# Audio tower on one core: the last token tile's values by seven half-size products, and the token sums of the next group moved forward

## The chip, the core and the metric

The kernel runs on one core of a Trainium2 chip. A core has TensorE (PE, matrix products), VectorE (DVE), ScalarE (ACT), GpSimd (POOL) and SyncE (SP, which here only issues transfers). The engines run side by side, each in the order of its own instructions, and wait for one another through semaphores. The metric is the device time of one execution in microseconds (us).

## The reference, cut to what matters

64 clips of 80000 samples are cut into 157 frames of 512. A cosine transform makes `h` (64 x 157 x 512). Then come one attention layer and one layer of 16 experts, all in 32-bit floats:

```python
h = einsum('bfh,kh->bfk', frames, D)              # the tokenizer
x = layernorm(h)
key_phase = tanh(x @ Wk + bk) * pi                # query_phase alike
V = x @ Wv + bv
# phases and positions give causal weights over the tokens of one clip;
# V is summed with them, and gate = sigmoid(x @ Wg + bg) mixes the two sums
h = h + x + (total / norm) @ Wo + bo
y = layernorm(h)
# the mean of y over a clip's tokens chooses one of 16 experts for the clip
h = h + gate * (y @ We[idx] + be[idx])
```

The change concerns `V = x @ Wv + bv` alone, for some of the tokens.

## The kernel before, in words

**Groups and tiles.** The 64 clips go through in 16 groups (`g`) of four. A clip's 157 tokens are padded to 160, so a group has 640 token columns. They make five tiles: `n` = 0 to 3 with 128 columns each (32 tokens of each of the four clips), and a fifth, `TAIL`, which also has 128. The transposed input `xT` keeps them as two halves of 320 columns: half 0 holds tiles 0 and 1 and 64 columns of `TAIL`, half 1 the other 64 columns of `TAIL` and then tiles 2 and 3.

**Products.** A 512 x 512 weight on two halves of tokens is cut into two by two blocks, and the eight block products are replaced by seven (Strassen's scheme). `weight_sums` (L370) makes the sums of weight blocks once, `factors` (L384) names them 1 to 7. `token_sums` (L399) makes four sums of token blocks for each group, as a generator that stops after each sum: sum 0 (L411) and sum 2 (L414) on POOL or DVE, sums 1 and 3 (L99) always on DVE. `product` (L437) is one of the seven on 256 tokens, eight rows in the profile (line L445). `gather` (L455) puts it where it belongs. The gate uses all 320 columns of a half (`gate_product`, L648). The values use 256 of 320: `TAIL` doesn't take part in the seven, and is done by `value` (L486) with `by_tokens` (L247, matmuls L250): four matmuls with 512 columns. `keep_value` (L490) adds the bias `bv` on its way out (L100, DVE). Each row of a 32-bit matmul in the profile is one of two passes, so four matmuls are eight rows.

**Column tiles.** Where the stationary operand has 32 columns only, four matmuls stand side by side in the array, each on 32 of the 128 output partitions: the projection to phases (`project`, L594, matmuls L601), the scores (L689) and the experts (L953).

**Order.** It is written out by hand: each engine does its instructions in the order of the program. For each group from 1 on: `project_and_values` (L1098), `gate` (L1153), `experts_and_embedding` (L1171), `attention` (L1197). In the first, the projection is followed on PE by product 1, the tail values, and products 2, 6, 7, 5, 4, 3. Between them stand the steps that route the clips of the group before: `move_blocks` (L795) issues sixteen transfers, ten from SP and six from POOL, of the transposed tokens; `xsum`, `route`, `route_own`, `route_all`, `pick` make the choice on DVE; `fetch` (L893) issues four indirect loads of 1 MB from POOL. `fold_phases` (L611) and `phasors` (L615) turn the projected phases into sines on DVE and ACT. `add_bv` (L513) adds the bias to the values of tiles 0 to 3 on POOL.

**Where the token sums of the next group were made.** `attention(g)` ends with the output product, during which `scale_all` (L344) scales the next group's `xT`, with statistics (DVE, then POOL: L237 to L244), with the normalisation (`normal2`, ACT), then `value_sums(g + 1)` (L1190), which makes sums 0 and 2 on POOL, and `turn_blocks` (L787, DVE transposes) around two experts of the group before (`expert`, L973, with L964 on DVE). Sums 1 and 3 follow in the next `project_and_values`, behind `value`.

**Accumulators.** The pool of PSUM tiles has four buffers of two banks, taken in turn. Products 2, 4 and 3 are accumulated onto the buffers of 1, 7 and 5 (`ONTO`).

Of the kernel before, what the change touches and what calls it, by code (L numbers as in the profile page):

```python
# [17 lines left out]
ALU = mybir.AluOpType  # L18
# [4 lines left out]
P = 128  # L23
# [30 lines left out]
def audio_tower(ctx: ExitStack, tc: tile.TileContext, a, out):  # L54
# [36 lines left out]
    def psum():  # L91

        return ps_mm.tile([P, 2, 512], F32, tag="mm", name="mm")
# [153 lines left out]
    def by_tokens(ps, x, n, w):  # L247

        for c in range(C):
            nc.tensor.matmul(ps, tile_of(x[:, c], n), w[:, c, :], start=(c == 0), stop=(c == C - 1))  # L250
        return ps
# [73 lines left out]
    def add_bo(g, n):  # L325
        r = S[g]["res"][n]
        nc.gpsimd.tensor_tensor(r, r, bo, ALU.add)  # L327
# [16 lines left out]
    def scale_all(g):  # L344

        s = S[g]
        if g == 0:
            scale = psum()
            lo = 0

            for n in (0, 1, TAIL, TAIL, 2, 3):
                rows = slice(0, P) if n != TAIL else slice(0, HT) if lo < HN - 1 else slice(HT, P)
                m, at = divmod(lo, HN)
                w = rows.stop - rows.start
                nc.tensor.transpose(
                    scale[:, m, at : at + w], s["rstd", n][rows].to_broadcast([w, P]), ident[rows, rows]
                )
                lo += w
        else:
            scale = s.pop("scale")  # L360
        for m in range(2):
            x = half(s["xT"], m)
            nc.vector.tensor_tensor(x, x, scale[:, m, :HN].unsqueeze(1).to_broadcast([P, C, HN]), ALU.mult)
# [112 lines left out]
    def value_buffer(g, n):  # L476

        s = S[g]
        if n == TAIL:
            s["v", n] = p1.tile([P, D], F32, tag="v_t", name="v_t")  # L480
        else:
            s["v2", n // 2] = v = p1.tile([P, 2, D], F32, tag="v", name="v", bufs=2)
            for b in range(2):
                s["v", n + b] = v[:, b, :]

    def value(g, n):  # L486
        s = S[g]
        s["vps", n] = by_tokens(psum()[:, 0, :], s["xT"], n, wv)

    def keep_value(g, n):  # L490
        s = S[g]
# [21 lines left out]
    def add_bv(g, m, of=slice(0, D)):  # L513
        v = S[g]["v2", m][:, :, of]
        by = bv[:, of].unsqueeze(1).to_broadcast([P, 2, of.stop - of.start])
        nc.gpsimd.tensor_tensor(v, v, by, ALU.add)  # L516
# [255 lines left out]
    def normal2(g, n):  # L772
        s = S[g]
        if n == TAIL:
            x = p1.tile([P, D], F32, tag="v_t", name="x2_t")
        else:
            if n % 2 == 0:
                s["x22"] = p1.tile([P, 2, D], F32, tag="v", name="x2", bufs=2)
            x = s["x22"][:, n % 2, :]
        rstd, shift = s.pop(("st2", n))  # L780
        if at_end(g, n):
            nc.vector.tensor_scalar(x, s["res"][n], shift, rstd, ALU.subtract, ALU.mult)
        else:
            nc.scalar.activation(x, s["res"][n], AF.Identity, bias=shift, scale=rstd)  # L784
        s["x2", n] = x

    def turn_blocks(g, n):  # L787

        s = S[g]
        if n == TAIL:  # L790
            s["blocks2"] = p1.tile([P, C * GB, LP], F32, tag="gT", name="turned2")
        to = s["blocks2"].rearrange("p (q c) t -> p c q t", c=C)[..., Q * n : Q * (n + 1)]
        nc.vector.transpose(to, s.pop(("x2", n)).rearrange("p (c q t) -> p c q t", c=C, q=GB))
# [179 lines left out]
    def expert(g, n, between=lambda c: None):  # L973
        ps = psum()
        for c in range(C):
            between(c)
            expert_chunk(g, n, c, ps[:, 0, :])
        between(C)
        expert_out(g, n, ps[:, 0, :])
# [118 lines left out]
    def project_and_values(g):  # L1098

        project(g)  # L1100
        made = S[g].pop("made")
        if g == 1:
            turn_blocks(0, TAIL)
            turn_blocks(0, 2)
        fold_phases(g)
        if g == 1:
            turn_blocks(0, 3)
        value_product(g, 1)
        keep_product(g)
        if g == 1:  # L1110
            normal2(0, 0)
            normal2(0, 1)
        value(g, TAIL)
        next(made)
        if g == 1:
            for n in (2, 3, TAIL):
                add_bo(g, n)
            turn_blocks(0, 0)
        else:
            next(made)  # L1120
        keep_value(g, TAIL)
        if g == 1:
            turn_blocks(0, 1)
        moves = move_blocks(g - 1)
        next(moves)
        S[g - 1]["late"] = xsum(g - 1, 2 * Q, L)
        value_product(g, 2)
        keep_product(g)
        add_bv(g, 0, slice(0, H))
        next(moves)  # L1130
        phasors(g)
        value_product(g, 6)
        keep_product(g)
        route(g - 1)
        value_product(g, 7)
        keep_product(g)
        route_own(g - 1)
        value_product(g, 5)
        keep_product(g)
        if g == 1:  # L1140
            next(made)
        fold_once(g + 1, 0)
        value_product(g, 4)
        keep_product(g)
        route_all(g - 1)
        pick(g - 1)
        fetch(g - 1)
        value_product(g, 3)
        keep_product(g)
        weigh()  # L1150
        fold_twice(g + 1, 0)

    def gate(g):  # L1153
        ahead = g + 1 < NG
        for i in (1, 6, 2, 7, 5, 4, 3):
            gate_product(g, i)
            if i == 1:
                pick_gate(g - 1)
                bias(g - 1)
                fold_once(g + 1, 1)  # L1160
                add_bv(g, 0, slice(H, D))
                add_bv(g, 1)
            if i == 5:
                if not ahead:
                    scores(g)
                fold_twice(g + 1, 1)
            for n in {6: (0,), 2: (1,), 3: (2, 3, TAIL)}.get(i, ()) if ahead else ():
                embed(g + 1, n)
                embed_statistics(g + 1, n)
# [20 lines left out]
    def value_sums(g):  # L1190

        S[g]["blocks"] = halves(S[g]["xT"])
        S[g]["made"] = made = token_sums(g, engine=nc.gpsimd)
        next(made)
        next(made)

    def attention(g):  # L1197
        ahead = g + 1 < NG
        if ahead and g > 0:
            for n in (0, 1, 2):  # L1200
                add_bo(g + 1, n)
        if g == 0:
            for _ in weight_sums(wg, t_g, nc.gpsimd):
                pass
        for c in range(C):
            read(g, c)
            if ahead and g > 0:
                for n in ((), (3, TAIL), (), ())[c]:
                    add_bo(g + 1, n)
        S[g]["blocks"] = halves(S[g]["gT"])  # L1210
        made = token_sums(g, tail=False)
        if g == 0:
            for n in (0, 1):
                add_bo(1, n)
        for i in (1, 2, 6, 7, 5, 4, 3):
            output_product(g, i)
            if i == 1:
                for _ in range(4 if g else 3):
                    next(made)
                if g == 0:  # L1220
                    scale_all(1)
                output_tail(g)
                statistics2(g, (TAIL,))
            elif i == 6:
                normal2(g, TAIL)
            elif i == 7 and g == 0:
                next(made)
            elif i == 5 and g == 0:
                value_sums(1)
            elif i == 5 and ahead:  # L1230
                scale_all(g + 1)
        for of in ((0, 1),) if ahead else ((0,), (1,)):
            statistics2(g, of)
        normal2(g, 2)
        normal2(g, 3)
        if not ahead:
            normal2(g, 0)
        elif g > 0:
            normal2(g, 0)
            normal2(g, 1)  # L1240
            value_sums(g + 1)
            for n in (TAIL, 2, 3):
                turn_blocks(g, n)
            expert(g - 1, 2)
            for n in (0, 1):
                turn_blocks(g, n)
            expert(g - 1, 3)

    for g in range(NG):
        if g == 0:  # L1250
            first_values()
            first_gate()
        else:
            project_and_values(g)
            gate(g)
            if g + 1 < NG:
                experts_and_embedding(g)
            else:
                S[g]["rwg"] = rwg = p2.tile([P, C, Q], F32, tag="sines", name="rwg")
                nc.sync.dma_start(out=rwg, in_=a["rwg"])  # L1260
        attention(g)
# [160 lines left out]
```

## Time and profile before

| | us |
|---|---|
| median of three runs | 1302.68 |
| the runs | 1301.87 to 1304.14 |
| the profiled execution | 1301.98 |
| its span, first to last instruction | 1300.0 |
| PE busy | 1293.2 (99%) |
| DVE busy | 1023.6 (79%) |
| POOL busy | 592.7 (46%) |
| ACT busy | 431.9 (33%) |

The busy time of an engine counts from the first to the last of the instructions that overlap, so it tells that PE always had something in flight, not that each was at its best rate. The chain of work that ended last runs over PE for 97% of the span. The page is followed by groups of instructions (by line, engine and shape), waits (who waited for whom) and a timeline in order of time.

### The profile page before, as it was taken

How to read it: one execution, taken by the hardware profiler on the slowest of the kernel's cores; microseconds unless marked ns; L12 is line 12 of the kernel's file. 1: busy time of each engine (PE TensorE's matmuls, PEld its weight loads, DVE VectorE, ACT ScalarE, POOL GpSimd, SP SyncE). 2: the span in 40 equal slices, each digit the busy share in tenths (PEclk: the TensorE clock that was granted, in tenths of full speed). 3: DMA queues.
4: the chain of work that ended last, by engine and by line, in shares of the span. 5: the costliest groups of instructions: out<-in, count | busy, mean ns of one | idle time of the engine just before them, and what ended most of it. 6: DMA issues, size and time to landing. Idle time of an engine off the chain costs nothing.

```text
span 1300.0 us, 26072 instructions
## 1 busy us (share of the span) xinstructions
PE 1293.2 (99%) x10152; PEld 864.7 (67%) x10152; DVE 1023.6 (79%) x2056; ACT 431.9 (33%) x768; POOL 592.7 (46%) x781
## 2 busy tenths in 40 slices
PE   9999999999999999999999999999999999999998
PEld 5677666676666767666676666766666676666762
DVE  6888787878877887788878878788778877888583
ACT  2525334142432324334242331424323243342410
POOL 2356445344553446435444453446434454354424
PEclk9999999999999999999999999999999999999999
DMA  7015224252442425323252342424323262241506
GB/s 242 1 52 178 76 61 173 61 171 75 114 147 54 152 75 177 93 57 146 80 183 76 77 174 49 166 75 131 128 64 145 75 193 77 58 154 36 181 9 210
DMA packets 60578, 144.46 MB, mean 111 GB/s; under 512 B 14136, under 2 KB 31432, under 8 KB 52520
## 3 DMA queue, kind: packets, MB, share of 16 engines
q1 hardware_dynamic: 45620, 62.68, 17.6%
q0 software_dynamic: 14336, 79.47, 17.2%
q8 instruction: 81, 1.33, 0.4%
q10 hardware_dynamic: 500, 0.64, 0.2%
q14 instruction: 41, 0.34, 0.1%
HBM read 102.47 MB, written 20.62 MB: 95 GB/s over the span
## 4 chain that ended last, share of the span: by engine, by line
PE 97%; DMA 1%; POOL 1%; issue 0%; SPq 0%; DVE 0%; POOLq 0%
PE mm L445 29%; PE mm L953 20%; PE mm L658 17%; PE mm L250 10%; PE mm L705 9%; PE mm L270 3%; PE mm L272 3%; PE mm L601 3%; PE mm L637 1%; PE mm L689 1%; DMA tables<-in_table_sums 1%; DMA t_v<-in_we,rows 1%; PE mm L201 0%; PE mm L219 0%; PE mm L684 0%
## 5 line engine op out<-in xcount | busy, mean ns | idle before, releaser
L953 PE MATMUL mm<-we,x2T 128*32 128x512 f32 x2400 | 263.8, 593 | 0.0
L953 PEld LDWEIGHTS mm<-we,x2T 128*32 128x32 f32 x2400 | 75.0, 110 | 165.6 <-issue 165.5
L237 POOL TENSOR_SCALAR rstd<-mv 128x2 f32<-128x2 f32 (+1 forms) x50 | 11.7, 235 | 241.0 <-DVE mv L233 240.9
L516 POOL TENSOR_TENSOR v<-v,bv 128x512 f32<-128x512 f32 (+1 forms) x45 | 72.7, 1632 | 101.2 <-ACT v L465 101.2
L705 PE MATMUL mm<-att,v 32*128 32x320 f32 (+3 forms) x2048 | 113.2, 357 | 0.0
L705 PEld LDWEIGHTS mm<-att,v 32*128 32x128 f32 x2048 | 94.6, 185 | 22.0 <-issue 12.6
L784 ACT ACTIVATE x<-res,shift,rstd 128x512 f32<-128x512 f32 x61 | 46.4, 807 | 172.7 <-POOL shift L244 171.9
L327 POOL TENSOR_TENSOR res<-res,bo 128x512 f32<-128x512 f32 x64 | 95.7, 1514 | 13.1 <-ACT res L323 13.0
L100 DVE TENSOR_TENSOR gT<-mm,gT 128x320 f32<-128x320 f32 (+3 forms) x128 | 71.2, 566 | 31.7 <-PE mm L658 28.7
L712 DVE TENSOR_TENSOR gT<-mm,gT 128x320 f32<-128x320 f32 x128 | 59.5, 485 | 42.4 <-PE mm L705 42.3
L237 POOL TENSOR_SCALAR dev<-mv 128x5 f32<-128x5 f32 (+1 forms) x20 | 4.9, 244 | 188.7 <-DVE mv L233 188.1
L232 DVE BATCH_NORM_STATS2 st<-res 128x6 f32<-128x512 f32 x128 | 87.9, 686 | 3.3
L445 PE MATMUL mm<-t_o,sum 128*128 128x256 f32 x384 | 85.5, 379 | 0.0
L445 PE MATMUL mm<-t_v,sum 128*128 128x256 f32 x360 | 80.1, 379 | 0.0
L445 PEld LDWEIGHTS mm<-t_o,sum 128*128 128x128 f32 x384 | 73.0, 190 | 9.9
L676 ACT ACTIVATE gT<-gT,hbg 128x320 f32<-128x320 f32 (+1 forms) x90 | 45.6, 554 | 100.1 <-DVE gT L100 100.1
L323 ACT ACTIVATE res<-res,shift,more 128x512 f32<-128x512 f32 x64 | 46.9, 803 | 87.2 <-POOL more L313 87.2
L907 POOL DMA_INDIRECT we<-in_we,rows x60 | 59.9, 998 | 34.4 <-DVE rows L903 20.4
L445 PEld LDWEIGHTS mm<-t_v,sum 128*128 128x128 f32 x360 | 68.4, 190 | 9.3
L250 PE MATMUL mm<-wv,xT 128*128 128x512 f32 x160 | 71.8, 592 | 0.0
L658 PE MATMUL mm<-sum,wg 128*128 128x320 f32 (+1 forms) x240 | 69.2, 431 | 0.0
L658 PE MATMUL mm<-xT,wg 128*128 128x317 f32 x240 | 68.9, 430 | 0.0
(223 smaller groups left out, 2832.3 us busy)
## 6 DMA issues: line engine op xcount, KB each, us to landing
xT<-in_frames SPq DMA_DIRECT2D x32, 640.0 KB
out<-res SPq DMA_DIRECT2D x236, 64.0 KB
x2T<-turned SPq DMA_DIRECT2D x150, 80.0 KB
x2T<-turned POOLq DMA_DIRECT2D x90, 80.0 KB, 1.9
scale<-row SPq DMA_DIRECT2D x15, 320.0 KB
out<-res_t SPq DMA_DIRECT2D x62, 32.0 KB
out<-res_t SPq DMA_DIRECT2D x62, 26.0 KB
wg<-in_wg SPq DMA_DIRECT2D x1, 1024.0 KB
```

What stands on the lines that cost most here:

```text
L100: add = lambda *x: nc.vector.tensor_tensor(*x, ALU.add)
L232: nc.vector.bn_stats(st, h)
L250: nc.tensor.matmul(ps, tile_of(x[:, c], n), w[:, c, :], start=(c == 0), stop=(c == C - 1))
L323: nc.scalar.activation(s["res"][n], s["res"][n], AF.Identity, bias=shift, scale=more)
L327: nc.gpsimd.tensor_tensor(r, r, bo, ALU.add)
L445: nc.tensor.matmul(ps[:, b, :], lhs[:, c, P * b : P * (b + 1)], w[:, c, :], start=(first and c == 0), stop=(c == 1), skip_group_check=not ...
L516: nc.gpsimd.tensor_tensor(v, v, by, ALU.add)
L658: nc.tensor.matmul(ps[:, o, :width], w[:, c, o * P : (o + 1) * P], rhs[:, c, :width], start=(first and c == 0), stop=(c == 1), skip_group_ ...
L705: nc.tensor.matmul(to, s["v", n][q, c * P : (c + 1) * P], by, start=(n == 3), stop=(n == TAIL))
L712: nc.vector.tensor_tensor(th, r[:, :, 0], th, ALU.mult)
L907: nc.gpsimd.indirect_dma_start(out=ws[b][:, n * k : n * (k + 1)], out_offset=None, in_=of, in_offset=bass.IndirectOffsetOnAxis(ap=rows[:, ...
L953: nc.tensor.matmul(ps[Q * i : Q * (i + 1), :], s["x2T"][:, c, i, Q * n : Q * (n + 1)], s["ws"][i][:, c, :], start=(c == 0), stop=(c == C - 1),
```

## The change

For groups 2 to 15 the tail tile's 128 columns are taken as two halves of 64 tokens, and go through the same seven products as the rest. `value_tail` stands directly behind the projection, ahead of product 1. A product has 64 tokens, given as two stationary blocks of 32 columns; two products (1 and 5; 6 and 7; 2 and 3) or the two column halves of product 4 are issued in turn, so that they fill the four column tiles of the array. Products 2 and 3 are accumulated onto 1 and 5, after ACT has copied these two out. The other sums are made on DVE in place in the SBUF tile `v_t`, the last block is copied by ACT. The bias is added to `v_t` later, on POOL, in `gate`.

All four token sums of the next group are made within `attention`: sum 0 right behind `scale_all`, sums 2 and 1 behind `normal2`, sum 3 behind the last `turn_blocks`. In groups 2 to 15 product 6 now comes before product 2. Group 1 keeps the old order in a function of its own.

```diff
+    def value_tail(g):
+        s = S[g]
+        value_buffer(g, TAIL)
+        v, ends, mids = s["v", TAIL], psum(), psum()
+        top, low = slice(0, HT), slice(HT, P)
+        left, right = slice(0, H), slice(H, D)
+
+        def part(i, rows, to, cols=left, first=False):
+            x, w = operand(g, i), fac_v[i]
+            x = x[:, :, :HT] if i in (4, 7) else x[:, :, 2 * P :]
+            for c in range(2):
+                for k in (0, Q):
+                    yield nc.tensor.matmul(
+                        to[rows.start + k : rows.start + k + Q],
+                        x[:, c, k : k + Q],
+                        w[:, c, cols],
+                        start=(first and c == 0),
+                        stop=(c == 1),
+                        skip_group_check=True,
+                    )
+
+        def together(*parts):
+            for _ in zip(*parts):
+                pass
+
+        to = ends[:, 0, :H]
+        together(part(1, top, to, first=True), part(5, low, to, first=True))
+        for rows in (top, low):
+            nc.scalar.copy(v[rows, right], to[rows])
+        fourth = mids[:, 1, :P]
+        together(*(part(4, rows, fourth, slice(P * n, P * (n + 1)), True) for n, rows in enumerate((top, low))))
+        both = mids[:, 0, :H]
+        together(part(6, top, both, first=True), part(7, low, both, first=True))
+        together(part(2, top, to), part(3, low, to))
+        add(v[top, right], both[top], v[top, right])
+        add(v[low, left], both[low], v[top, right])
+        add(v[low, right], v[low, right], v[low, left])
+        for n, rows in enumerate((top, low)):
+            half_row = v[low, P * n : P * (n + 1)]
+            add(half_row, fourth[rows], half_row)
+        add(v[top, right], to[low], v[top, right])
+        nc.scalar.copy(v[top, left], to[top])

     def project_and_values(g):
         project(g)
         made = S[g].pop("made")
-        if g == 1:
-            turn_blocks(0, TAIL)
...
         fold_phases(g)
...
+        value_tail(g)
         value_product(g, 1)
         keep_product(g)
-        value(g, TAIL)
-        next(made)
-        if g == 1:
...
-        else:
-            next(made)
-        keep_value(g, TAIL)
...
         moves = move_blocks(g - 1)
         next(moves)
         S[g - 1]["late"] = xsum(g - 1, 2 * Q, L)
+        value_product(g, 6)
+        keep_product(g)
+        route(g - 1)
         value_product(g, 2)
         keep_product(g)
         add_bv(g, 0, slice(0, H))
         next(moves)
         phasors(g)
-        value_product(g, 6)
-        keep_product(g)
-        route(g - 1)
         value_product(g, 7)
...
 # gate(g), behind product 1
                 add_bv(g, 1)
+                if g > 1:
+                    v = S[g]["v", TAIL]
+                    nc.gpsimd.tensor_tensor(v, v, bv, ALU.add)
...
 # value_sums(g): the first of the sums alone
         S[g]["made"] = made = token_sums(g, engine=nc.gpsimd)
-        next(made)
         next(made)
...
 # attention(g)
             elif i == 5 and g == 0:
                 value_sums(1)
+                next(S[1]["made"])
             elif i == 5 and ahead:
                 scale_all(g + 1)
+                value_sums(g + 1)
...
             normal2(g, 0)
             normal2(g, 1)
-            value_sums(g + 1)
+            next(S[g + 1]["made"])
+            next(S[g + 1]["made"])
             for n in (TAIL, 2, 3):
                 turn_blocks(g, n)
             expert(g - 1, 2)
             for n in (0, 1):
                 turn_blocks(g, n)
+            next(S[g + 1]["made"])
             expert(g - 1, 3)
```

More of the change, by code (lines that the diff above doesn't have):

```diff
@@ L1101, in project_and_values, with second_values @@
         made = S[g].pop("made")
-        if g == 1:
-            turn_blocks(0, TAIL)
-            turn_blocks(0, 2)
         fold_phases(g)
-        if g == 1:
-            turn_blocks(0, 3)
+        value_tail(g)
         value_product(g, 1)
         keep_product(g)
-        if g == 1:
-            normal2(0, 0)
-            normal2(0, 1)
+        moves = move_blocks(g - 1)
+        next(moves)
+        S[g - 1]["late"] = xsum(g - 1, 2 * Q, L)
+        value_product(g, 6)
+        keep_product(g)
+        route(g - 1)
+        value_product(g, 2)
+        keep_product(g)
+        add_bv(g, 0, slice(0, H))
+        next(moves)
+        phasors(g)
+        value_product(g, 7)
+        keep_product(g)
+        route_own(g - 1)
+        value_product(g, 5)
+        keep_product(g)
+        fold_once(g + 1, 0)
+        value_product(g, 4)
+        keep_product(g)
+        route_all(g - 1)
+        pick(g - 1)
+        fetch(g - 1)
+        value_product(g, 3)
+        keep_product(g)
+        weigh()
+        fold_twice(g + 1, 0)
+    def second_values(g):
+        project(g)
+        made = S[g].pop("made")
+        turn_blocks(0, TAIL)
+        turn_blocks(0, 2)
+        fold_phases(g)
+        turn_blocks(0, 3)
+        value_product(g, 1)
+        keep_product(g)
+        normal2(0, 0)
+        normal2(0, 1)
         value(g, TAIL)
         next(made)
[L1115 to L1118, printed above, removed]
-        else:
-            next(made)
+        for n in (2, 3, TAIL):
+            add_bo(g, n)
+        turn_blocks(0, 0)
         keep_value(g, TAIL)
-        if g == 1:
-            turn_blocks(0, 1)
+        turn_blocks(0, 1)
         moves = move_blocks(g - 1)
@@ L1139, in project_and_values @@
         keep_product(g)
-        if g == 1:
-            next(made)
+        next(made)
         fold_once(g + 1, 0)
@@ L1253, in audio_tower @@
         else:
-            project_and_values(g)
+            (second_values if g == 1 else project_and_values)(g)
             gate(g)
```

## The prediction, made before the changed kernel ran

> **What bounds the kernel now.** I read the page's busy shares first, then who PE waited for, then PE in order of time in a middle group, then the groups by shape for prices, then ACT and DVE in the same stretch.
>
> The page, busy times and PE by slices:
>
> ```profile
> PE 1293.2 (99%) x10152; PEld 864.7 (67%) x10152; DVE 1023.6 (79%) x2056; ACT 431.9 (33%) x768; POOL 592.7 (46%) x781
> ...
> PE   9999999999999999999999999999999999999998
> ```
>
> All waits of PE's matmuls in the whole execution:
>
> ```profile
> PE mm L191 <- POOL ident masks.py:199: 1.4, 1, 1.4
> PE mm L953 <- DMA spare<-in_we,rows: 0.3, 1, 0.3
> PE mm L219 <- DMA tables<-in_table_sums: 0.3, 1, 0.3
> PE mm L201 <- DMA wv<-in_wv: 0.2, 1, 0.2
> PE mm L953 <- DMA t_v<-in_we,rows: 0.2, 1, 0.2
> ```
>
> They sum to 2.4 us, none in groups 1 to 14. PE never waits there, so what PE streams sets the end, and a microsecond taken from it is a microsecond of the kernel unless a new wait returns it.
>
> PE's timeline in one middle group (start, us, rows):
>
> ```profile
> 567.22 2.34 PE L601 MATMUL mm<-xT,wkq 128*32 128x320 f32 x32
> 569.49 1.99 PE L445 MATMUL mm<-wv,xT 128*128 128x256 f32 x8
> 571.32 3.60 PE L250 MATMUL mm<-wv,xT 128*128 128x512 f32 x8
> 574.75 1.89 PE L445 MATMUL mm<-wv,xT 128*128 128x256 f32 x8
> 576.48 5.34 PE L445 MATMUL mm<-t_v,sum 128*128 128x256 f32 x24
> ```
>
> Differences of starts are PE's time. L250, the tail's values, takes 574.75 - 571.32 = 3.43 us: 8 passes of 512 columns, 0.429 each, 1.2 columns per ns. A product (8 passes of 256) takes 576.48 - 574.75 = 1.73, 0.216 a pass, the same rate. Every row's own length is some 0.17 longer, because rows overlap.
>
> Does PE reach this rate with 32-column tiles too? By shape (last numbers: busy, mean ns of one row):
>
> ```profile
> L953 PE MATMUL mm<-we,x2T 128*32 128x512 f32 x2400 | 263.8, 593 | 0.0
> L250 PE MATMUL mm<-wv,xT 128*128 128x512 f32 x160 | 71.8, 592 | 0.0
> L601 PE MATMUL mm<-xT,wkq 128*32 128x320 f32 x512 | 37.4, 433 | 0.0
> L689 PE MATMUL mm<-qf,kf 128*32 128x128 f32 x128 | 6.5, 276 | 0.0
> ```
>
> It does. L953's 2400 rows take 263.8: four at a time 0.440, as one full-width pass of L250 (71.8 / 160 = 0.449). L601's 32 rows take 2.27 us in the timeline, 8 sets of four at 0.284 against 320 / 1.2 = 0.267. The scores (L689), whose sets are as short as 32 columns, run from 526.24 to 527.07: 0.83 us for 480 columns twice, 960 / 1.2 = 0.80. So neither weight loads nor short rows cost anything here.
>
> **What the skill says.** The Trainium skill, "TensorE: Matmul & The Clock Gate", Part 3, has matmuls in different column tiles run concurrently, with 2.38 times measured for three tiles; the rows above show close to four for four. "TensorEngine Tiling (Array Packing)", Key Properties: changing the tiling mode drains TensorE. The trace agrees: L601 to L445 costs about (2.27 - 2.13) + (1.83 - 1.71) = 0.26 us, while L250 to L445 costs 0.02. "PSUM", Terms: two engines must not be on the same bank and quadrant at once; the change keeps to it by making products 2 and 3 wait for ACT's copies. No run here shows a collision.
>
> **The change part by part, per group (14 groups, 2 to 15).**
>
> PE removes 3.43 us. It adds products of 64 tokens, two at a time: (1, 5) is 8 matmuls in 2 sets of four, times 2 passes: 4 sets of rows with 256 columns, 4 x 256 / 1.2 = 0.853; product 4 in halves 4 sets of 128, 0.427; (6, 7) 0.853; (2, 3) 0.853; sum 2.99. `value_tail` follows L601 in the same mode, and the exit of 0.26 us, now paid ahead of product 1, stays one exit. Net -0.44 us a group.
>
> Waits of PE within the new stretch. I count from the projection's start (567.22 = 0); its stream ends at 2.17. (1, 5) runs to 3.02, 4 to 3.45, (6, 7) to 4.30, (2, 3) to 5.16. Products 2 and 3 wait for two ACT copies of 64 x 256 out of product 1's and 5's bank. ACT and DVE rows around it:
>
> ```profile
> 569.62 0.53 ACT L609 ACTIVATE u<-mm,bkq 128x320 f32<-128x320 f32 x1 [1.23 <-PE mm L601]
> 571.52 0.58 ACT L463 COPY v<-mm 128x512 f32<-128x512 f32 x1 [1.37 <-PE mm L445]
> 590.69 0.27 ACT L292 COPY sines<-mm 128x129 f32<-128x129 f32 x1 [0.77 <-PE mm L272]
> 590.85 0.65 ACT L293 COPY res<-mm 128x256 f32<-128x256 f32 x1
> ...
> 570.18 0.49 DVE L613 SCALAR_TENSOR_TENSOR u<-u 128x320 f32<-128x320 f32 x1 [0.41 <-ACT u L609]
> 570.59 0.82 DVE L99 TENSOR_TENSOR sum<-sum,xT 128x640 f32<-128x640 f32 x1
> 571.45 0.82 DVE L99 TENSOR_TENSOR sum<-xT,sum 128x640 f32<-128x640 f32 x1
> 574.95 0.69 DVE L100 TENSOR_TENSOR v_t<-mm,bv 128x512 f32<-128x512 f32 x1 [2.68 <-PE mm L250]
> ```
>
> ACT is done with the tanh at 2.93. A copy of 256 columns, between 129 (0.27) and 512 (0.58), is 0.38; the skill's "ScalarE: Activation LUTs", What ACT_TABLE_LOAD costs, gives an estimate of 0.186 + 256 x 0.833 ns = 0.40. The first starts when (1, 5) has drained, 3.02 + 0.17 + 0.04 = 3.23 (L463 starts 0.2 after its product's stream); both end by 3.95. PE wants them at 4.30, its weight load 0.13 earlier: 0.2 us to spare. At L293's price, a strided copy of 0.65, both would end at 4.5, and PE would lose 0.3. I take 0.38, since the new copies are contiguous like L463, and keep the other end for the range.
>
> DVE: one add of 0.69 (L100) goes; four adds of 256 columns (0.43, the price of L837's 128x256) and two of 128 (0.28) come, 2.3 in all, +1.6 us. Sums 1 and 3 (0.82 each) move ahead of the projection. So the transposes and L964 come 0.8 to 1.6 later, `fold_phases` ends near 4.6 instead of 3.4. PE's dependence on this: product 4 needs the accumulator that L964 of tile 2 frees (1.15 of 3.02), product 3 needs sum 3 (about 3.5 of 4.3), product 6 L964 of tile 3 (4.2 of 7.1). The adds run from 4.6 to 7.0, where DVE sat idle for 2.68 us. The last ACT copy and L463 behind it end by 7.9; product 2, which wants L463, starts at 8.8.
>
> POOL: sum 0 (L411 in two pieces, 1.70) moves from 566.8 to 560.4, when `scale_all` ends; POOL's next statistics came at 562.9, so it fits by 0.7. Sum 2 then ends at 1.35 on the count above, and product 7 wants it at 3.45. The bias on `v_t` adds 1.27 behind `add_bv` in the gate, and is wanted by the attention 20 us later. `add_bv` of product 2 and POOL's six transfers (3.1) come 1.2 later, since 6 now precedes 2; they end near 15.7, and the next on POOL (L122) started at 16.3. The indirect loads follow `pick`, which is tied to product 4 and moves with PE. Phasors end near 16.7; `weigh` wants them at 19.3. SP's ten transfers keep their place behind eight output transfers, which L964's delay pushes by about 1.6; L684, 33 us later, reads them. All these edits I cost at nothing: PE's own stream hides them.
>
> Sum: 3.43 - 2.99 = 0.44, times 14 = 6.2 us. In the profiled execution the span goes from 1300.0 to 1293.8 and the time from 1301.98 to 1295.8. That execution is 0.70 below the median of the runs, so the median goes to 1302.68 - 6.2 = 1296.5.
>
> **The rivals.**
>
> (a) Chance 0.76: the sum above, with up to a third of it lost to small waits: 1296.5, own range 1295.5 to 1298.6.
>
> (b) Chance 0.12: ACT's copies come late, for L293's price or because the wait keeps PE from loading weights ahead. A loss of 0.3 to 0.45 a group leaves 0 to 2 us: 1300.7 to 1302.7, no measurable change. For it: the margin is 0.2 us. Against: L463 and L465 start within 0.2 us of their product's end and take 0.58 for twice the columns.
>
> (c) Chance 0.08, slower: column tiles of two products don't overlap as the expert's do. Here the tiles are issued in the order 0, 64, 32, 96, and two products with separate operands alternate. If only two of four ran together, the stretch would take 5.97, +2.54 a group, +35.6: 1338. The point of decision is 3.43 / 7 = 0.49 us for a set pair instead of 0.427, 15% of overlap lost. Against: L953 and L601 have separate operands in their tiles as well, at the full rate.
>
> (d) Chance 0.04: the 0.44 us gained is given back at a later wait, the expert weights for L684 above all. The loads issued at 586.25 to 590.2 landed in at most 11.6 us, so by 602, PE wanted them at 604.87: 3 us to spare against 0.44. If it were so, 1302.7.
>
> **How the numbers follow.** About 0.2% (2.6 us) is what a measurement of this kernel can tell from no change. Faster by more (below 1300.1): (a) and a little of (b), 0.80. Within: the rest of (b), and (d), 0.11. Slower: (c) and what other stall I have not seen, 0.09. The range runs from 1295.4, a little under (a), to 1301.5 in (b); it leaves out (c), part of (b) and (d), under 2 in 10.
>
> **What would show it.** After: 14 stretches between L601 and product 1 of 2.99 us in 64 rows of 128*32, no PE wait in the groups, a span near 1293.8. A wait of the new matmuls on ACT's copy means (b). New rows that start in pairs, and a stretch near 6 us, mean (c). Waits of L684 on transfers mean (d). The prediction would be wrong if DVE, with 1.6 us more a group, came late with sum 3 or L964, which PE's waits on DVE would tell.

## The result, and the profile after

The changed kernel takes 1296.18 us (median of six runs, 1295.61 to 1296.97) against 1302.28 us for the kernel before (1301.19 to 1304.14) in runs on the same chip: a ratio of 0.9951, 95% interval 0.9939 to 0.9964. That is 6.1 us, or 0.5%. The profiled execution has a time of 1295.61 and a span of 1293.8.

The page of the changed kernel, busy times and PE by slices:

```profile
PE 1287.2 (99%) x10936; PEld 871.3 (67%) x10936; DVE 1042.9 (81%) x2126; ACT 445.8 (34%) x810; POOL 617.5 (48%) x795
...
PE   9999999999999999999999999999999999999998
```

PE is busy for 6.0 us less although it has 784 rows more. DVE, ACT and POOL are busy for 19, 14 and 25 us more, and the end didn't move with them.

All waits of PE's matmuls:

```profile
PE mm L191 <- POOL ident masks.py:199: 1.4, 1, 1.4
PE mm L219 <- DVE even L100: 0.4, 1, 0.4
PE mm L997 <- DMA t_v<-in_we,rows: 0.2, 1, 0.2
```

None is in groups 1 to 14, and none belongs to the new matmuls (L503). PE in one middle group (two lines that begin within 0.02 us of each other are the two products of a pair, each on two column tiles):

```profile
565.32 2.34 PE L645 MATMUL mm<-xT,wkq 128*32 128x320 f32 x32
567.47 0.39 PE L503 MATMUL mm<-wv,xT 128*32 128x256 f32 x2
567.48 0.39 PE L503 MATMUL mm<-t_v,sum 128*32 128x256 f32 x2
...
568.33 0.62 PE L503 MATMUL mm<-t_v,xT 128*32 128x128 f32 x16
568.77 1.05 PE L503 MATMUL mm<-t_v,sum 128*32 128x256 f32 x16
569.63 0.39 PE L503 MATMUL mm<-wv,xT 128*32 128x256 f32 x2
569.65 0.39 PE L503 MATMUL mm<-wv,sum 128*32 128x256 f32 x2
...
570.61 1.99 PE L445 MATMUL mm<-wv,xT 128*128 128x256 f32 x8
572.44 1.89 PE L445 MATMUL mm<-t_v,sum 128*128 128x256 f32 x8
...
643.62 2.34 PE L645 MATMUL mm<-xT,wkq 128*32 128x320 f32 x32
```

The next group's projection in the kernel before:

```profile
645.93 2.34 PE L601 MATMUL mm<-xT,wkq 128*32 128x320 f32 x32
```

Products 1 and 5 take 0.86 us, product 4 0.44, 6 and 7 0.86, 2 and 3 0.98 with a part of the exit from the 32-column mode in it. From the projection's start to the end of product 1 are 572.44 - 565.32 = 7.12 us, where it was 574.75 - 567.22 = 7.53 with the old tail.

The best measure is the distance from one group's projection to the next, because it has no start-up and no end in it: here 643.62 - 565.32 = 78.30 us; before, the projections stood at 567.22 and 645.93, 78.71. In each kernel's trace it is the same for groups 2 to 14 to within 0.01 us (but for one period of one experiment, named below). The change is worth 0.41 us a group, 14 times: 5.7 us. The other 0.5 us of the span is outside. From the last group's projection to the end are 102.1 us instead of 103.1, which is 0.6 more than the 0.41 of that group; the first projection starts 0.1 us later (45.9 against 45.8). On the chain that ended last, the last expert weights (`t_v`) took 6.87 us from issue to use in this execution and 7.29 in that of the kernel before. Whether the change has a part in this wasn't tested. The start alone varies more: over the ten traces of this document the first projection starts between 45.5 and 47.8 us.

ACT and DVE of the same group:

```profile
567.72 0.53 ACT L653 ACTIVATE u<-mm,bkq 128x320 f32<-128x320 f32 x1 [0.75 <-PE mm L645]
568.58 0.76 ACT L519 COPY v_t<-mm 64x256 f32<-64x256 f32 x2 [0.34 <-PE mm L503]
572.48 0.36 ACT L532 COPY v_t<-mm 64x256 f32<-64x256 f32 x1 [3.14 <-DVE v_t L100]
572.75 0.58 ACT L463 COPY v<-mm 128x512 f32<-128x512 f32 x1
...
567.64 0.78 DVE L99 TENSOR_TENSOR sum<-xT,sum 128x640 f32<-128x640 f32 x1
569.95 0.88 DVE L100 TENSOR_TENSOR v_t<-mm,v_t 64x256 f32<-64x256 f32 x2 [0.47 <-PE mm L503]
571.39 1.05 DVE L100 TENSOR_TENSOR v_t<-mm,v_t 64x128 f32<-64x128 f32 x3
```

The two copies end at 569.34, and products 2 and 3, which wait for them, start at 569.63. Sum 3 ends at 568.42, 1.2 us ahead of product 3. DVE's adds run from 569.95 to 572.44, and L463 ends at 573.33, ahead of product 2 at 574.17.

### The profile page after: what moved, and what is told of

Read it like the earlier page. It is cut to its first block, busy times and chain, and to the rows that moved or that the text cites. A ratio compares the mean times of both kernels' runs of the same rounds, so it can differ in the third digit from the quotient of the medians.

```text
span 1293.8 us, 27807 instructions
## 1 busy us (share of the span) xinstructions
PE 1287.2 (99%) x10936; PEld 871.3 (67%) x10936; DVE 1042.9 (81%) x2126; ACT 445.8 (34%) x810; POOL 617.5 (48%) x795
## 4 chain that ended last, share of the span: by engine, by line
PE 97%; DMA 1%; POOL 1%; issue 1%; DVE 0%; SPq 0%; DVEq 0%; POOLq 0%
PE mm L445 29%; PE mm L997 20%; PE mm L702 17%; PE mm L749 9%; PE mm L250 6%; PE mm L503 3%; PE mm L270 3%; PE mm L272 3%; PE mm L645 3%; PE mm L681 1%; PE mm L733 1%; DMA t_v<-in_we,rows 1%; DMA wv<-in_wv 0%; PE mm L201 0%; PE mm L219 0%
## 5 line engine op out<-in xcount | busy, mean ns | idle before, releaser
L749 PE MATMUL mm<-att,v 32*128 32x320 f32 (+3 forms) x2048 | 113.2, 357 | 0.0
L749 PEld LDWEIGHTS mm<-att,v 32*128 32x128 f32 x2048 | 94.6, 185 | 22.0 <-issue 12.6
L411 POOL TENSOR_TENSOR sum<-xT 128x512 f32<-128x512 f32 (+1 forms) x30 | 25.8, 882 | 105.1 <-DVE xT L363 102.5
L237 POOL TENSOR_SCALAR rstd<-mv 128x2 f32<-128x2 f32 (+1 forms) x50 | 18.5, 370 | 114.6 <-DVE mv L233 114.5
```

What stands on the lines that cost most here:

```text
L749: nc.tensor.matmul(to, s["v", n][q, c * P : (c + 1) * P], by, start=(n == 3), stop=(n == TAIL))
```

## The experiments

My theory: PE's stream sets the end; the seven products make it shorter by 0.41 us a group; the sums made sooner, the place behind the projection and product 6 ahead of 2 earn nothing by themselves, but each keeps a wait or a change of mode off PE that would cost most of the gain or more. The main rivals: that the moved sums or the new order gave part of the gain (the first experiment), that they don't matter (the next three), and that the overlap of the tiles or ACT's copies are a limit (the last ones). Each time is set beside the kernel before in runs on the same chip. The period is the distance between two projections in a middle group; it is 78.71 before and 78.30 after.

| | us | before, same chip | ratio, 95% interval | period, us |
|---|---|---|---|---|
| sums sooner, old tail | 1303.19 | 1302.30 | 1.0008 [1.0001, 1.0015] | 78.71 |
| seven products, old sums | 1309.04 | 1302.30 | 1.0055 [1.0038, 1.0071] | 79.12 |
| product 2 ahead of 6 | 1311.07 | 1302.30 | 1.0074 [1.0057, 1.0091] | 79.34 |
| tail behind product 1 | 1301.49 | 1302.30 | 0.9991 [0.9982, 1.0000] | 78.64 |
| products one after the other | 1296.60 | 1302.06 | 0.9958 [0.9941, 0.9975] | 78.33 |
| one copy more | 1299.36 | 1302.06 | 0.9979 [0.9970, 0.9989] | 78.49 |
| three copies more | 1311.00 | 1302.06 | 1.0070 [1.0053, 1.0087] | 79.28 |
| 64-column tiles | 1299.50 | 1302.06 | 0.9983 [0.9972, 0.9994] | 78.45 |

**The sums sooner, with the old tail.**

```diff
         fold_phases(g)
-        value_tail(g)
+        value(g, TAIL)
+        keep_value(g, TAIL)
         value_product(g, 1)
...
-                if g > 1:
-                    v = S[g]["v", TAIL]
-                    nc.gpsimd.tensor_tensor(v, v, bv, ALU.add)
```

> One part alone: all token sums made within the attention before, product 6 ahead of product 2, but the tail values by four matmuls of 512 columns as before, directly behind the projection, with the bias added on the way out. Theory (PE's stream sets the end, the sums moved sooner only make room): PE streams what it streamed before, 3.43 us for the tail, so 1302.3, within 1 us of the kernel before. Rival (a part of the 6.1 us came from the sums or from the new order of 6 and 2): between 1296.2 and 1301.

It took 1303.19 us, and the period is that of the kernel before to the hundredth, 78.71. The 0.9 us that it is slower are in none of the groups 2 to 14. In its profiled execution, whose span is 2.3 us longer than the kernel before's, the first projection starts at 47.8 us instead of 45.8, so the loads at the start are the likely place; the run with 64-column tiles below starts as late. The other executions have no trace to show it. Moving the sums and product 6 earns nothing. PE's timeline shows the same stretch as before with its parts in another order:

```profile
569.26 2.34 PE L645 MATMUL mm<-xT,wkq 128*32 128x320 f32 x32
571.53 3.70 PE L250 MATMUL mm<-wv,xT 128*128 128x512 f32 x8
575.07 1.89 PE L445 MATMUL mm<-wv,xT 128*128 128x256 f32 x8
576.79 1.89 PE L445 MATMUL mm<-t_v,sum 128*128 128x256 f32 x8
```

From 569.26 to 576.79 are 7.53 us, as from 567.22 to 574.75 before.

**The seven products, with the sums where they were.**

```diff
         fold_phases(g)
+        next(made)
+        next(made)
         value_tail(g)
...
                 scale_all(g + 1)
-                value_sums(g + 1)
...
-            next(S[g + 1]["made"])
+            value_sums(g + 1)
             next(S[g + 1]["made"])
...
-            next(S[g + 1]["made"])
             expert(g - 1, 3)
```

> The other part alone: the seven products of the tail behind the projection, product 6 ahead of 2, but the token sums of groups 2 to 15 made where they were: 0 and 2 on POOL behind the normalisation, 1 and 3 on DVE behind fold_phases. Theory: products 6 and 7 then wait for sum 1, which DVE ends about 4.2 us after the projection's start, where PE wants it at 3.45; with the semaphore and the weight load PE loses 0.85 us a group, more than the 0.41 that the seven products save: 14 x (0.85 - 0.41) = 6 us slower than before, 1308. Rival (the sums are ready in time anyway, or PE's wait is hidden): 1296.2.

It took 1309.04, and a period of 79.12: 0.82 us a group more than the change, 0.41 more than the kernel before. DVE and PE in its trace, around the wait:

```profile
572.30 0.82 DVE L99 TENSOR_TENSOR sum<-sum,xT 128x640 f32<-128x640 f32 x1
...
571.94 0.62 PE L503 MATMUL mm<-t_v,xT 128*32 128x128 f32 x16
573.17 1.07 PE L503 MATMUL mm<-t_v,sum 128*32 128x256 f32 x16 [0.61 <-DVE sum L99]
```

Sum 1 ends at 573.12 and products 6 and 7 start 0.05 later; in the changed kernel they start 0.44 after product 4 does (568.33, 568.77), here 1.23. So the seven products alone lose; what makes them pay is that the sums are there.

**Product 2 ahead of product 6.**

```diff
-        value_product(g, 6)
-        keep_product(g)
-        route(g - 1)
         value_product(g, 2)
         keep_product(g)
         add_bv(g, 0, slice(0, H))
         next(moves)
         phasors(g)
+        value_product(g, 6)
+        keep_product(g)
+        route(g - 1)
```

> The change with product 2 ahead of product 6, as it was before. Theory: product 2 goes onto product 1's bank and waits for ACT's copy of it (L463), which now stands behind the tail's last copy, and that behind DVE's adds. In the changed kernel L463 ends at 573.33, 0.89 us after product 1's stream (572.44); with semaphore and weight load PE waits 1.0 us a group: 14 us, 1310. Rival (the order of 6 and 2 does not matter for PE): 1296.2.

It took 1311.07, a period of 79.34, 1.04 us a group over the change. ACT and PE of its trace:

```profile
577.69 0.36 ACT L532 COPY v_t<-mm 64x256 f32<-64x256 f32 x1 [3.14 <-DVE v_t L100]
577.96 0.58 ACT L463 COPY v<-mm 128x512 f32<-128x512 f32 x1
...
575.82 1.99 PE L445 MATMUL mm<-wv,xT 128*128 128x256 f32 x8
578.59 1.99 PE L445 MATMUL mm<-wv,xT 128*128 128x256 f32 x8 [0.78 <-ACT v L463]
```

Product 2 starts 0.05 us after L463's end at 578.54. So the wait is the one that was expected, but the reason given for it, the tail's last copy ahead of L463, is the small part. Product 1's last row ends at 577.81 (575.82 + 1.99). In the kernel before L463 begins 0.04 us after product 1's last row (571.48, 571.52); here that would be 577.85, and it began at 577.96, when the tail's last copy, which waits for the last of DVE's adds, was through. That copy accounts for 0.11 us. The rest is L463 itself: product 2 stands directly behind product 1, onto whose bank it goes, and the 0.58 us of the copy can't begin before product 1 is done. In the kernel before, the tail's 3.43 us stood between the two; in the changed kernel product 6 does.

**The tail behind product 1.**

```diff
         fold_phases(g)
-        value_tail(g)
         value_product(g, 1)
         keep_product(g)
+        value_tail(g)
```

> The change with the seven tail products behind product 1 instead of directly behind the projection, so that PE goes from 32-column tiles to full width, back, and again to full width: one entry and one exit more in each of 14 groups. Theory (a change of the array's mode costs PE time): an exit costs 0.2 to 0.26 us, an entry 0.1 to 0.25; 4 to 7 us more than the changed kernel, 1300 to 1303. Rival (the place does not matter, the 0.26 us seen at the exit is a wait of another kind): 1296.2.

It took 1301.49, a period of 78.64: 0.34 us a group over the change, 5.3 us over 1296.2. PE's timeline shows no idle time at the two extra changes (exit after the projection, entry to the tail; the exit after the tail is there in both):

```profile
567.73 2.34 PE L645 MATMUL mm<-xT,wkq 128*32 128x320 f32 x32
570.00 1.99 PE L445 MATMUL mm<-wv,xT 128*128 128x256 f32 x8
571.92 0.40 PE L503 MATMUL mm<-wv,xT 128*32 128x256 f32 x1
```

From the projection to product 1 are 2.27 us, instead of 2.15 from the projection to the tail in the changed kernel, and product 1 takes 1.92 instead of 1.73 for a product among its like. ACT's two copies end at 573.82, 0.29 us ahead of products 2 and 3 (574.11), as in the changed kernel, so the loss isn't theirs. "TensorEngine Tiling (Array Packing)", Key Properties, in the Trainium skill says that a change of tiling mode drains TensorE; if that is what these longer distances are, one exit and one entry cost 0.34 us here.

**The products one after the other.**

```diff
         def together(*parts):
-            for _ in zip(*parts):
-                pass
+            for part_ in parts:
+                for _ in part_:
+                    pass
```

> The change with the two products of a pair issued one after the other (all of 1, then all of 5, and so on) instead of in turn, so that matmuls next to each other in the program fill two of the four column tiles only. Theory (tiles overlap only where the neighbours in the program lie in different tiles): the stretch doubles from 3.02 to 6.04 us, 42 us more than the changed kernel, 1338. Rival (PE looks far enough ahead to start the second product's tiles while the first product's later matmuls wait for theirs): 1296 to 1298.

My theory was wrong. It took 1296.60, a period of 78.33, no different from the change but for 0.03 us. PE's timeline (the lines with `wv,xT` are product 1, those with `t_v,sum` product 5):

```profile
567.76 0.39 PE L503 MATMUL mm<-wv,xT 128*32 128x256 f32 x2
567.77 0.41 PE L503 MATMUL mm<-t_v,sum 128*32 128x256 f32 x2
567.97 0.39 PE L503 MATMUL mm<-wv,xT 128*32 128x256 f32 x2
568.01 0.39 PE L503 MATMUL mm<-t_v,sum 128*32 128x256 f32 x2
```

Product 5's first rows start 0.01 after product 1's, although all four matmuls of product 1, eight rows, stand ahead of them in the program, in its compiled form too, and six of these rows start later. So PE began product 5, whose tiles were free, past rows of product 1 that stood ahead of it and whose tiles were still in use.

**More copies on ACT.** One more (n = 1), and three more (n = 3), of the second of the two copies that products 2 and 3 wait for:

```diff
-        for rows in (top, low):
+        for rows in (top, low) + (low,) * n:
             nc.scalar.copy(v[rows, right], to[rows])
```

> The change with one copy more on ACT: the second of the two copies that products 2 and 3 wait for is made twice. Theory (margin of the ACT copies): in the changed kernel the two copies end at 569.34 and products 2 and 3 start at 569.63; the two are 0.39 us apart, so a third ends at 569.73, PE follows 0.05 later and has 0.1 of weight load uncovered: a loss of 0.15 to 0.25 us in each of 14 groups, 1298.3 to 1299.8. Rival (the margin is wider, other work of PE fills the gap): 1296.2.

> The same with three copies more. Theory: the last ends at 570.5, a loss of 0.9 to 1.05 us in each of 14 groups, 1309 to 1311, and PE's waits name ACT's copy. Rival: 1296.2, or a smaller loss than the copies' own length, if PE has other work to do.

1299.36 with one, 1311.00 with three; the periods are 0.19 and 0.98 us over the change, both within what was expected. ACT and PE, first with one more, then with three more:

```profile
569.44 1.16 ACT L519 COPY v_t<-mm 64x256 f32<-64x256 f32 x3 [0.33 <-PE mm L503]
...
569.63 1.05 PE L503 MATMUL mm<-t_v,sum 128*32 128x256 f32 x16
570.65 0.40 PE L503 MATMUL mm<-wv,xT 128*32 128x256 f32 x1
```

```profile
574.08 1.95 ACT L519 COPY v_t<-mm 64x256 f32<-64x256 f32 x5 [0.34 <-PE mm L503]
...
574.27 1.05 PE L503 MATMUL mm<-t_v,sum 128*32 128x256 f32 x16
576.09 0.40 PE L503 MATMUL mm<-wv,xT 128*32 128x256 f32 x1 [0.77 <-ACT v_t L519]
```

The copies end at 570.60 and 576.03, and PE follows 0.05 and 0.06 later. With one more, products 2 and 3 start 1.02 us after 6 and 7, instead of 0.86, and no wait is named: so short a wait shows only in the distance. One copy of 0.39 uses the whole margin up and costs half of itself; each further one costs its full length, (0.98 - 0.19) / 2 = 0.40. From 0.19 = 0.39 - margin the margin is 0.20 us, which is what the prediction had reckoned. (One period of the run with three copies, from group 12's projection to group 13's, is longer by 0.17; the time is lost some 56 us behind the projection, in L749 of the attention, so not at the copies. What held it there is open.)

**64-column tiles.** Each product's 64 tokens as one stationary block:

```diff
-                for k in (0, Q):
+                for k in (0,):
                     yield nc.tensor.matmul(
-                        to[rows.start + k : rows.start + k + Q],
-                        x[:, c, k : k + Q],
+                        to[rows],
+                        x[:, c],
```

> The change with each product's 64 tokens as one stationary block of 64 columns instead of two of 32: half as many matmuls, two tiles of 64 columns in the array instead of four of 32, the same columns streamed. Theory (changing the array's mode costs, the number of tiles does not): the stretch itself stays 3.0 us, but the projection before it is in 32-column tiles, so there is one more change of mode, 0.1 to 0.26 us in each of 14 groups: 1297.6 to 1299.8. Rival (fewer and larger blocks are as good or better): 1295.5 to 1296.4.

It took 1299.50, a period of 78.45, 0.15 us a group over the change. PE's timeline:

```profile
567.92 2.34 PE L645 MATMUL mm<-xT,wkq 128*32 128x320 f32 x32
570.19 0.43 PE L503 MATMUL mm<-wv,xT 128*64 128x256 f32 x1
570.20 0.43 PE L503 MATMUL mm<-t_v,sum 128*64 128x256 f32 x1
570.46 0.38 PE L503 MATMUL mm<-wv,xT 128*64 128x256 f32 x1
```

The first row of the tail starts 2.27 us after the projection instead of 2.15, and the tail's first pass takes 0.27 instead of 0.22; after that the rates are the same. By its place this is the price of one more change of mode, from 32 to 64 columns. Half as many instructions gained nothing.

No run came out better than the change.

## Why the prediction was right

**The bound.** "PE never waits there, so what PE streams sets the end" held. The sums sooner with the old tail left the period at 78.71 with another order on PE, DVE and POOL, and the change moved it by what PE lost, while three engines got busier.

**PE's sum.** The forecast was 3.43 - 2.99 = 0.44 us a group; the period moved by 0.41. The mis-sized term is the 2.99: it took the new stretch at 1.2 columns per ns, and the old one from the trace, where a pass takes 0.429 for 512 columns and 0.216 for 256, a little longer than the 0.427 and 0.213 of that rate. At 0.215 a pass of 256 columns, as the changed kernel's rows follow each other, the stretch is 0.86 + 0.44 + 0.86 + 0.86 = 3.02, and the difference 0.41. The span nevertheless fell by the 6.2 us that were forecast, because 0.5 us came from outside the groups, which the sum didn't have. So the closeness of 1296.5 to 1296.18 is in part luck.

**One exit from the mode, not two.** Held, and measured: one more exit and entry cost 0.34 us. The price of 0.26 for the exit was a little high, because it was set against 1.2 columns per ns. Against the distances that the changed kernel shows without a change of mode it is (2.27 - 2.15) + (1.83 - 1.73) = 0.22 in the kernel before, and as much, (0.98 - 0.86) + (1.83 - 1.73), in the changed one.

**ACT's copies and the 0.2 us to spare.** Held: two copies of 0.37, together 0.76, against 0.72 forecast (from 3.23 to 3.95; the second doesn't overlap the first), and a margin of 0.20 by the run with one copy more. Rival (b) needed copies of 0.65. It wasn't far: one copy too many takes half of the gain.

**DVE.** The adds were forecast from 4.6 to 7.0 on the count from the projection's start and ran from 4.63 to 7.12; L463 was to end by 7.9 and ended at 8.01, product 2 started at 8.85 (forecast 8.8). Sum 3 was to be done at 3.5 and was at 3.10. POOL's six transfers were to end near 15.7, and did at 15.79 (577.97 + 3.14); L122, behind them, didn't start late.

**Rival (c), tiles that don't overlap.** Its premise was wrong twice over: the pairs overlap fully, and issued in a row they did so too.

**Rival (d), a later wait.** Nothing of it: L684 of before (L728 after) waits for no transfer.

## What to carry to other kernels

Where PE has no gap, price a rewrite by passes and columns from rows of the same tile mode, and then ask of each operand and accumulator by how much it comes before PE wants it; here three margins (0.2 us at ACT's copies, 0.8 at L463 ahead of product 2, 1.2 at sum 3) carried a gain of 0.41 us, and undoing one of the moves around them lost 0.34 to 1.04 us a group. Put work in a small-tile mode next to other work in the same mode. For effects of a few tenths of a per cent compare the period of a group in the trace, since start and end vary more than the effect.

## What the runs showed of the hardware that I had not expected

That each engine works in the order of its own instructions, as the description of the core has it, is not so for PE across column tiles: with all of product 1's matmuls ahead, product 5's, in other tiles, began 0.01 us after it, and the order of issue cost 0.03 us a group. How far it looks ahead wasn't tried beyond the four matmuls of one product. A change from 32-column to 64-column tiles costs PE about half (0.15 us) of an exit to full width and an entry back (0.34).
